# Cross attention on one Trainium2 core: seven block products in float32 replaced by three float32r products

## The chip, the core and the metric

The kernel runs on one core of a Trainium2 chip. The core has a matrix engine (TensorE, PE in the profile, with its weight loads listed apart as PEld), three engines for elementwise work (VectorE or DVE, ScalarE or ACT, GpSimd or POOL), a queue engine that issues DMA (SyncE or SP), an on-chip memory (SBUF) and eight accumulation banks (PSUM) of 512 float32 per partition. Each engine works through its own list of instructions in order and waits on semaphores for the others. The metric is the device time in microseconds of one execution; lower is better.

## The reference

For each of 32 batches, x and y are 256 channels by 1024 positions:

```python
x_q = jnp.einsum('oc,bcn->bno', w_qk, y)
x_k = jnp.einsum('oc,bcn->bon', w_qk, x)
x_v = jnp.einsum('oc,bcn->bon', w_v, x) + b_v[None, :, None]
energy = jnp.einsum('bnc,bcm->bnm', x_q, x_k)
attention = jax.nn.softmax(energy, axis=-1)
attention = attention / (1e-07 + attention.sum(axis=1, keepdims=True))
x_r = jnp.einsum('bcn,bnm->bcm', x_v, attention)
x_r = jax.nn.relu(jnp.einsum('oc,bcn->bon', w_t, x - x_r) + b_t[None, :, None])
return x + x_r
```

The energies are a 1024 by 1024 table per batch. Each row gets a softmax, then each column is divided by its sum S over the rows (plus 1e-7).

## The kernel before

Weights are folded once: G = w_qk^T w_qk is applied to x alone ("keys", tile `gf`), so that energy = y^T (G x); w_v and w_t are folded into one matrix, so that u = (w_t w_v x)^T ("values", tile `ut`). The output is then relu(w_t x - u attention + b_t) + x.

TensorE works in two ways. The energies use *float32r* operands, which the array multiplies in one pass at reduced precision; each operand is split into a high part, a low part and a mixed part (class `Split`, lines 243 to 282: `yf` and `gf`, three forms each), and three products are summed in PSUM. A row tile of 128 rows by 1024 columns takes 12 matmuls of 512 columns. All other products are full float32, which the profile shows as two matmul records each. To save some of them, keys, values and attention are computed by a scheme of seven block products instead of eight (class `Seven`, lines 293 to 350, with `Keys`, `Values` and `Attention`): the 2 by 2 blocks of each operand are added into sums (`summed`, `factors`, `mix`, `lefts`), and the seven products are combined afterwards (`combine`).

The order on PE, DVE, ACT and POOL is the order of the program text: class `InOrder` (line 62) chains each instruction behind the last one of its engine. DMA issues of SP are placed by the scheduler. One batch goes so:

- Energy, 8 row tiles n (lines 712 to 740): `first` and `second` on PE, `scaled` on ACT between them (it multiplies the sum of the first two forms in place by a constant), the row minimum `nm` on DVE, the exponential on ACT into the SBUF tile `e`, which holds all 8 rows, and `share` on DVE, which adds e times 1/rowsum into the column sums `acc`.
- Keys and values of the next batch (lines 742 to 767), then `columns` and `inverse` (lines 631 to 658), which turn `acc` into 1/S along the columns (tile `rc`).
- Attention (`Attention.run`, lines 557 to 595): `normal` multiplies all of `e` by 1/rowsum and by 1/S on DVE, `mix` forms the block sums `et` on DVE, PE multiplies them by `ur` (from `ut`, with sums `us` made on POOL), together with w_t times x (`xpart`), and DVE combines, adds x and stores.

Forms of the next batch's y and keys are made by ACT and by accumulating DMAs issued from POOL (`lower`, `mixed`), block sums of x by accumulating DMAs too (`summed`).

Of the kernel before, what the change touches and what calls it, by code (L numbers as in the profile page):

```python
# [17 lines left out]
def kernel(  # L18
# [11 lines left out]

# [12 lines left out]
    BIG = 3.0e38  # L53
    UP = 4096.0
    UNDER = 1.0 - 2.0**-13
    OVER = 1.0 + 2.0**-12

    const = ctx.enter_context(tc.tile_pool(name="const", bufs=1))
    xp = ctx.enter_context(tc.tile_pool(name="xp", bufs=2))
    ps_m = ctx.enter_context(tc.tile_pool(name="ps_m", bufs=1, space=bass.MemoryType.PSUM))  # L60

# [16 lines left out]
    pe, dve, act, pool = (InOrder(g) for g in (nc.tensor, nc.vector, nc.scalar, nc.gpsimd))  # L78

    banks = ps_m.tile([P, 8, MB], F32, name="banks")  # L80

    def bank(j):
        return banks[:, j]

    loaded = {}

    def load(b, pieces=1):
        to = xp.tile([P, KC, N], F32, tag="x", name=f"x_{b}")
        from_ = x[b].rearrange("(k p) n -> p k n", p=P)
        W = KC // pieces  # L90
        for j in range(pieces):
            nc.sync.dma_start(to[:, ts(j, W)], from_[:, ts(j, W)])
        loaded[b] = to

    def quarters(from_):

        return from_.rearrange("(k p) (h n) -> p k h n", p=P, h=MH)

    def corners(from_):

        q = quarters(from_)[:, 0, 0, :]
        return bass.AP(
            tensor=q.tensor, offset=q.offset, ap=[q.ap[0], [P * N + MB, 2], q.ap[-1]]
        )

    def accumulate(into, from_):
# [4 lines left out]
    ep = ctx.enter_context(tc.tile_pool(name="ep", bufs=1))  # L111
    scratch = ep.tile([P, 2, HT, MB], F32, tag="et", name="scratch").rearrange(
        "p j t m -> p (j t) m"
    )

    def room(j):
        return scratch[:, j, : KC * C].rearrange("p (k c) -> p k c", k=KC)

    wqk, wv, wt = room(0), room(1), room(2)
    ident = scratch[:, 3, :P]  # L120
    bv = scratch[:, 4, :KC].rearrange("p (k o) -> p k o", o=1)
    bvs = scratch[:, 5, : KC * P].rearrange("p (k n) -> p k n", k=KC)
    bt = const.tile([P, KC, 1], F32, name="bt")
    nbt = const.tile([P, KC, 1], F32, name="nbt")
    bu = const.tile([P, KC, P], F32, name="bu")
    for k, start in enumerate((nc.sync.dma_start, act.dma_start)):
        start(wqk[:, k], w_qk[ts(k, P)])
    load(0, KC)
    nc.sync.dma_start(wt, w_t.rearrange("(k p) c -> p k c", p=P))
    nc.sync.dma_start(bv, b_v.rearrange("(k p o) -> p k o", p=P, o=1))  # L130
    nc.sync.dma_start(wv, w_v.rearrange("(k p) c -> p k c", p=P))
    nc.sync.dma_start(bt, b_t.rearrange("(k p o) -> p k o", p=P, o=1))


    few = const.tile([P, P], F32, name="few")
    dve.memset(few, 0.0)
    behind = const.tile([P, 1], F32, name="behind")
    parts = const.tile([P, NB, NG + 1], F32, name="parts")
    dve.memset(parts[:, :, NG], EPS)
    idle = bank(7)  # L140
    for _ in range(5):
        pe.matmul(idle[:, :P], few, few, start=True, stop=True)
    make_identity(nc, ident)

    def lefts(name, ps, sign=1.0):


        w = const.tile([P, KC, C], F32, name=name)
        for k in range(KC):
            act.mul(w[:, k, :], ps[k][:, :C], sign)  # L150
        sums = const.tile([P, 4, P], F32, name=f"{name}s")
        s1, s2, s3, s4 = (sums[:, j] for j in range(4))

        def stt(out_, block, factor, other, op):
            dve.scalar_tensor_tensor(out_, block, factor * sign, other, ALU.mult, op)

        p11, p12, p21 = ps[0][:, :P], ps[1][:, :P], ps[0][:, P:C]
        a11, a12, a21, a22 = w[:, 0, :P], w[:, 1, :P], w[:, 0, P:], w[:, 1, P:]
        stt(s1, p21, 1.0, a22, ALU.subtract)
        stt(s3, p11, 1.0, a21, ALU.subtract)  # L160
        stt(s2, p11, -1.0, s1, ALU.add)
        stt(s4, p12, 1.0, s2, ALU.add)
        return w, (a11, a12, s4, a22, s1, s2, s3)


    pg = [bank(3 + i) for i in range(KC)]
# [5 lines left out]
    _, g_left = lefts("g", pg, UP)  # L172

    for k in range(KC):
        dve.tensor_scalar(bvs[:, k], few, bv[:, k], None, ALU.add)

    def turned_weights():

        pt = [bank(6 + i) for i in range(KC)]
        for i in range(KC):  # L180
            for k in range(KC):
                pe.transpose(pt[i][:, ts(k, P)], wt[:, k, ts(i, P)], ident)
        return lefts("wtT", pt)

    def value_weights(wtT):

        pw = [bank(4 + i) for i in range(KC)]
        for i in range(KC):
            for k in range(KC):
                pe.matmul(  # L190
                    pw[i][:, :C], wv[:, k, ts(i, P)], wtT[:, k, :], start=(k == 0), stop=(k == KC - 1)
                )
        return lefts("wvtT", pw, -1.0)[1]

    def value_bias(wtT):

        pb = bank(6)
        for k in range(KC):
            pe.matmul(pb[:, :C], bvs[:, k], wtT[:, k, :], start=(k == 0), stop=(k == KC - 1))
        act.mul(bu.rearrange("p k c -> p (k c)"), pb[:, :C], -1.0)  # L200
        act.mul(nbt[:, :, 0], bt[:, :, 0], -1.0)

    up = ctx.enter_context(tc.tile_pool(name="up", bufs=2))
    one = ctx.enter_context(tc.tile_pool(name="one", bufs=1))
    cp = ctx.enter_context(tc.tile_pool(name="cp", bufs=2))
    rowp = ctx.enter_context(tc.tile_pool(name="rowp", bufs=4))
    sp = ctx.enter_context(tc.tile_pool(name="sp", bufs=4))

    def temp(tag, name):
        return cp.tile([P, MB], F32, tag=tag, name=name)  # L210

    def matmul(into, lhs, rhs, onto=False):
        pe.matmul(into, lhs, rhs, start=not onto, stop=True, skip_group_check=onto)

    def value(v):

        return v.bitcast(F32)

    def summed(b):

        s = up.tile([P, 4, MB], F32, tag="xs", name=f"xs_{b}")
        t1, t3, t4, t2 = (s[:, j] for j in range(4))
        to = loaded[b]
        b11, b12 = to[:, 0, ts(0, MB)], to[:, 0, ts(1, MB)]
        b21, b22 = to[:, 1, ts(0, MB)], to[:, 1, ts(1, MB)]
        if b == 0:
            pool.tensor_tensor(t1, b11, b12, ALU.add)
            pool.tensor_tensor(t2, b22, t1, ALU.add)
            pool.tensor_tensor(t3, b12, b22, ALU.add)
            pool.tensor_tensor(t4, b21, t2, ALU.add)  # L230
            steps = []
        else:
            q = quarters(x[b])
            nc.sync.dma_start(s[:, :2], q[:, 0, 1:2, :].to_broadcast([P, 2, MB]))
            nc.sync.dma_start(s[:, 2:], q[:, 1])
            steps = [
                lambda: accumulate(s[:, :2], corners(x[b])),
                lambda: accumulate(s[:, 2:], s[:, 0:1].to_broadcast([P, 2, MB])),
                lambda: accumulate(t4, q[:, 1, 1]),
            ]  # L240
        return (b11, b21, b22, t4, t1, t2, t3), steps

    class Split:


        def __init__(self, name, b, by):
            self.name, self.b, self.by = name, b, by
            self.to = one.tile([P, 3, KC, N], F32R, tag=name, name=f"{name}_{b}")
            self.rows = {}

        def row(self, i):
            if i not in self.rows:
                self.rows[i] = rowp.tile([P, N], F32, tag="row", name=f"{self.name}r_{self.b}_{i}")
            return self.rows[i]

        def parts(self, i):

            high, low, both = (self.to[:, j, i] for j in range(3))
            act.mul(high, self.rows[i], UNDER * self.by)
            act.mul(low, value(high), -1.0 / self.by)  # L260
            act.mul(both, value(high), -1.0 / (UP * self.by))

        def high(self, i):
            act.mul(self.to[:, 0, i], self.rows[i], UNDER * self.by)

        def low(self, i):
            high, low = (self.to[:, j, i] for j in range(2))
            dve.scalar_tensor_tensor(
                low, value(high), -1.0 / self.by, self.rows[i], ALU.mult, ALU.add
            )  # L270

        def both(self, i):
            high, low, both = (self.to[:, j, i] for j in range(3))
            dve.scalar_tensor_tensor(
                both, value(high), -1.0 / (UP * self.by), value(low), ALU.mult, ALU.add
            )

        def lower(self, i):
            accumulate(value(self.to[:, 1, i]), self.rows[i])

        def mixed(self, i):
            accumulate(value(self.to[:, 2, i]), value(self.to[:, 1, i]))

# [196 lines left out]
    class Attention(Seven):  # L480
# [76 lines left out]
        def run(self, u, before=None, between=None):  # L557
# [7 lines left out]
            if u:  # L565
                u.c22()
# [288 lines left out]
```

## Time and profile before

| | |
|---|---|
| device time, median of 3 runs | 2095.8 us (2094.79 to 2096.62) |
| span of the profiled execution | 2094.2 us; no separate device time of that execution is given |
| TensorE clock granted | 0.999 of full |
| PE busy / PEld busy | 2080.7 / 1289.2 us |
| DVE / ACT / POOL busy | 1774.5 / 1145.9 / 674.7 us |
| DMA traffic | 306.04 MB, 170.68 MB of it in the queue that POOL feeds |

The span is the time from the first to the last instruction of one execution; a median a microsecond or two above it is the same time measured from outside. Busy time is the time in which an engine had a record open. In the profile `banks<-gf,yf` is an energy matmul, `banks<-e,ut`, `banks<-et,us`, `banks<-e,us` and `banks<-et,ut` are attention, `xs`, `x` with `g`, `gs` keys, with `wvtT`, `wvtTs` values, with `wtT`, `wtTs` the product w_t x. Nearly all lines read L73, because one helper issues every instruction; groups are told apart by their tiles.

### The profile page before, as it was taken

The page shows a single profiled execution, that of the slowest core. Times are in us where ns is not written, and L with a number is a line of the kernel's source. Part 1 is how long each engine was busy: PE and PEld are TensorE (multiplying, and loading weights), DVE is VectorE, ACT ScalarE, POOL GpSimd, SP SyncE. Part 2 cuts the span into 40 slices and gives each one's busy share as a digit, 9 for nine tenths or more (in the row PEclk, how much of TensorE's full clock was granted, in tenths as well). Part 3 has the DMA queues.
Part 4 walks back from the last instruction along what each step waited for, and adds up shares of the span by engine and source line. Part 5 has one row for each costly group of instructions (what it writes and reads, how often), then busy time and mean ns, then how long its engine had stood idle before and what let it go on. Part 6 is the DMA issues. An engine that isn't in the chain of part 4 may idle for free.

```text
span 2094.2 us, 21719 instructions
## 1 busy us (share of the span) xinstructions
PE 2080.7 (99%) x7586; PEld 1289.2 (62%) x7586; DVE 1774.5 (85%) x2264; ACT 1145.9 (55%) x1570; POOL 674.7 (32%) x574
## 2 busy tenths in 40 slices
PE   9999999999999999999999999999999999999998
PEld 6556666566665666556666556665566665666564
DVE  6898888998888988889888898888988888988898
ACT  5556554566455664546655556554566455664562
POOL 3322333323333133432333322333323333133321
PEclk9999999999999999999999999999999999999999
DMA  4766577665676656766558756577665776656740
GB/s 141 169 123 146 132 175 171 128 150 129 166 175 151 135 132 151 181 155 135 139 135 186 169 123 146 131 176 171 132 145 130 167 178 145 138 132 151 181 95 31
DMA packets 107789, 306.04 MB, mean 146 GB/s; under 512 B 10656, under 2 KB 11424, under 8 KB 107680
## 3 DMA queue, kind: packets, MB, share of 16 engines
q0 software_dynamic: 57040, 170.68, 44.5%
q1 hardware_dynamic: 50496, 133.85, 18.7%
q8 instruction: 60, 0.98, 0.2%
q14 instruction: 49, 0.40, 0.1%
q10 hardware_dynamic: 144, 0.13, 0.0%
HBM read 124.78 MB, written 33.55 MB: 76 GB/s over the span
## 4 chain that ended last, share of the span: by engine, by line
PE 72%; DVE 24%; issue 1%; DMA 0%; DVEq 0%; ACT 0%
PE banks L73 72%; DVE e L73 12%; DVE et L73 4%; DVE gfr L73 3%; DVE rc L73 2%; DVE sc L73 2%; DVE parts L73 1%; DVE acc L73 1%; DVE nm L73 0%; DMA gf<-gf 0%; DVEq L73 0%; DVE ri L73 0%; DVE z L73 0%; ACT ow L73 0%
## 5 line engine op out<-in xcount | busy, mean ns | idle before, releaser
L73 PE MATMUL banks<-gf,yf 128*128 128x512 f32 x3072 | 716.3, 394 | 0.3 <-DMA gf<-gf 0.3
L73 PEld LDWEIGHTS banks<-gf,yf 128*128 128x128 f32 x3072 | 576.2, 188 | 134.7 <-issue 15.5
L73 DVE TENSOR_REDUCE nm<-banks 128x1 f32<-128x1024 f32 x256 | 310.6, 1223 | 148.6 <-PE banks L73 136.1
L73 ACT ACTIVATE e<-banks,nm 128x1024 f32<-128x1024 f32 x256 | 287.0, 1121 | 134.5 <-DVE nm L73 134.5
L73 PE MATMUL banks<-et,us 128*128 128x512 f32 x768 | 353.9, 597 | 3.1 <-DVE et L73 1.4
L73 DVE SCALAR_TENSOR_TENSOR e<-e,ri,rc 128x512 f32<-128x512 f32 x512 | 347.4, 746 | 1.1
L73 ACT ACTIVATE banks<-banks 128x1024 f32<-128x1024 f32 (+1 forms) x288 | 264.1, 917 | 66.7 <-PE banks L73 66.6
L73 DVE SCALAR_TENSOR_TENSOR acc<-e,ri,acc 128x1024 f32<-128x1024 f32 x224 | 289.2, 1291 | 8.0
L73 PEld LDWEIGHTS banks<-et,us 128*128 128x128 f32 x768 | 143.2, 190 | 198.3 <-issue 161.7
L73 PE MATMUL banks<-e,ut 128*128 128x512 f32 x512 | 225.0, 592 | 0.9 <-DVE e L73 0.9
L73 POOL DMA_DIRECT2D yf<-yfr x62 | 53.1, 857 | 520.5 <-ACT yf L73 520.5
L73 ACT ACTIVATE z<-banks,bt 128x512 f32<-128x512 f32 x31 | 21.4, 689 | 338.5 <-DMA out_dram<-z 338.5
L73 PEld LDWEIGHTS banks<-e,ut 128*128 128x128 f32 x512 | 97.2, 190 | 123.7 <-issue 106.7
L73 DVE TENSOR_TENSOR et<-e 128x1024 f32<-128x1024 f32 x128 | 153.7, 1221 | 4.4
L73 POOL TENSOR_TENSOR ut<-ut,bu 128x1024 f32<-128x1024 f32 x64 | 154.6, 2501 | 0.3 <-ACT ut L73 0.3
L73 POOL DMA_DIRECT2D gf<-gf x62 | 53.1, 857 | 302.4 <-DMA gf<-gfr 257.7
L73 DVE SCALAR_TENSOR_TENSOR z<-z,x 128x512 f32<-128x512 f32 x96 | 134.6, 1403 | 3.3
L73 PE MATMUL banks<-e,us 128*128 128x512 f32 x256 | 125.3, 592 | 0.0
L73 ACT ACTIVATE gf<-gf 128x1024 fp32r<-128x1024 f32 x124 | 124.2, 1049 | 2.0
L73 ACT ACTIVATE yf<-yf 128x1024 fp32r<-128x1024 f32 x124 | 124.2, 1049 | 2.0
L73 POOL DMA_DIRECT2D xs<-xs x31 | 37.2, 1201 | 246.9 <-DMA xs<-in_x_dram 237.9
L73 PEld LDWEIGHTS banks<-wvtTs,xs 128*128 128x128 f32 x768 | 98.2, 192 | 29.6 <-issue 29.6
(104 smaller groups left out, 2617.0 us busy)
## 6 DMA issues: line engine op xcount, KB each, us to landing
yfr<-in_ctx_dram SPq DMA_DIRECT2D x64, 512.0 KB, 5.7
out_dram<-z SPq DMA_DIRECT2D x128, 256.0 KB, 3.5
x<-in_x_dram SPq DMA_DIRECT2D x31, 1024.0 KB, 7.5
xs<-in_x_dram SPq DMA_DIRECT2D x62, 512.0 KB, 5.0
yf<-yfr POOLq DMA_DIRECT2D x62, 512.0 KB, 5.2
yf<-yf POOLq DMA_DIRECT2D x62, 512.0 KB, 7.7
gf<-gfr POOLq DMA_DIRECT2D x62, 512.0 KB, 10.7
gf<-gf POOLq DMA_DIRECT2D x62, 512.0 KB, 5.2
```

The costliest lines, as they stand in the source:

```text
L73: self.last = getattr(self.engine, name)(*args, **kwargs)
```

## The change

The new kernel writes every product as three float32r products and drops the block scheme. Both operands of keys, values, w_t x, energy and attention now have three forms (HIGH, LOW, REST), and each product is HIGH x HIGH + REST x REST + LOW x LOW of suitably scaled forms, accumulated in one PSUM bank. Constants on either side carry the scales.

The division by S moves: attention multiplies u by the exponentials over the row sum alone, and 1/S is applied to the finished output columns (`divided`), together with a bias.

Exponentials stay in PSUM: `exp` writes in place over the energies, and the three forms of a row (`ef`, three buffers) and the column sum (`share`) are read from PSUM. Eight banks are four pairs: pairs 0 and 1 hold energy rows in turn (and keys and the first half of the values at the change of batch), pairs 2 and 3 the attention accumulators of the two output channel tiles (and the second half of the values, and w_t x). As attention no longer needs S, it follows the rows: after energy tile n, PE does attention of tile n - 2 (`attention`).

The forms of y are made per half of 512 positions (`Queries`), with two accumulating DMAs; those of x by ACT, POOL and one accumulating DMA per channel tile; those of keys and values out of PSUM by ACT and two DVE operations (`Right`); those of a row by ACT, DVE and one POOL addition (`low`). x is loaded a second time for the output.

The core of the diff, new code:

```python
class Right:                      # forms of keys and of values
    def high(self):
        act.mul(self.forms[0], self.p, 1.0 / UP)
    def low(self):
        dve.scalar_tensor_tensor(
            self.forms[1], value(self.forms[0]), -UP, self.p, ALU.mult, ALU.add)
    def rest(self):
        dve.scalar_tensor_tensor(
            self.forms[2], self.p, 1.0 / UP, value(self.forms[1]), ALU.mult, ALU.subtract)

# class Batch
def channels(self, p, w, i):      # keys(i) with gw, straight(c) with tw
    for h in range(MH):
        for j in ORDER:           # HIGH, REST, LOW
            for k in range(KC):
                matmul(p[:, h], w[:, j, k, ts(i, P)], self.xf[:, j, k, ts(h, MB)], ...)

def values(self, q):
    p = pair(2 if q else 3 if self.b == 0 else self.at)
    for t in range(HT):
        for j in ORDER:
            for k in range(KC):
                matmul(p[:, t // 2, ts(t % 2, C)], self.xf[:, j, k, ts(q * HT + t, P)], vw[:, j, k], ...)
...
def place(self, n):
    return pair((self.at + 1 + n) % 2)
def lowest(self, n):
    dve.tensor_reduce(low, flat(self.place(n)), AX.X, ALU.min)
def exp(self, n):
    p = flat(self.place(n))
    act.activation(p, p, AF.Exp, bias=self.row[n], scale=-1.0, accum_out=rs)
def high(self, n, h):
    act.mul(self.ef[n][:, HIGH, ts(h, MB)], self.place(n)[:, h], self.row[n])
def rest(self, n, h):
    dve.scalar_tensor_tensor(
        f[:, REST], self.place(n)[:, h], self.row[n], value(f[:, HIGH]), ALU.mult, ALU.subtract)
def scaled(self, n):
    act.mul(self.ef[n][:, LOW], value(self.ef[n][:, HIGH]), 1.0 / UP)
def low(self, n):
    pool.tensor_tensor(f[:, LOW], value(f[:, LOW]), value(f[:, REST]), ALU.add)
def share(self, n):
    for h in range(MH):
        dve.scalar_tensor_tensor(a, p[:, h], ri, a, ALU.mult, ALU.add)
def forms(self, n):
    for h in range(MH):
        self.high(n, h)
        self.rest(n, h)
    self.scaled(n)
    self.low(n)
def attention(self, n):           # 12 matmuls of 512 columns
    for c in range(KC):
        for h in range(MH):
            for j in ORDER:
                matmul(pair(2 + c)[:, h], u[:, j, ts(c, P)], self.ef[n][:, j, ts(h, MB)], ...)
def divided(self, c):
    dve.scalar_tensor_tensor(
        self.z[:, c], flat(pair(2 + c)), ubias[:, c], self.rc, ALU.add, ALU.mult)
...
# the row loop; what the turn of the batch does stands around it
for n in range(2, NT):
    if n > 2:
        cur.energy(n)
    cur.lowest(n)
    if n > 2:
        cur.share(n - 1)
    cur.exp(n)
    cur.recip(n)
    cur.forms(n)
    cur.attention(n - 2)
    if more and n == 2:
        nxt.x_high(0)
        nxt.x_rest(0)
    elif more and n == 3:
        nxt.x_high(1)
        nxt.x_rest(1)
        nxt.x_scaled(0)
    elif more and n == 4:
        nxt.x_scaled(1)
        nxt.x_low(0)
        nxt.x_low(1)
    if last and n == 5:
        last.relu(1)
        last.put(1)
```

In the turn, the order on PE is: attention 5, keys 0, attention 6, keys 1, attention 7, first half of the values, energy 0, second half of the values, w_t x for channel tile 0, energy 1, w_t x for tile 1, energy 2, attention 0, energy 3, and so on. On DVE it is: forms and share of row 7, `low` and `rest` of keys 0, `columns`, `inverse`, `low` and `rest` of keys 1, `divided` twice, then row 0 of the next batch with the forms of the values between its steps.

More of the change, by code (lines that the diff above doesn't have):

```diff
@@ L167 @@
+    ys = {}
+    cur = Batch(0)
+    for q in range(3):
+        ys[q] = Queries(q) if q < 2 else None
+    pg = [banks[:, i] for i in range(KC)]
     for i in range(KC):
@@ L207 @@
[L207 to L241, printed above, removed]
@@ L785 @@
[L785 to L824 removed]
+        nxt = Batch(b + 1)
@@ new lines @@
+        first = b == 0
+        v0 = cur.values(0)
+        v0.high()
+        if first or not more:
+            v0.low()
+        if first:
+            v1 = cur.values(1)
+        cur.energy(0)
+        cur.lowest(0)
+        if first:
+            v0.rest()
+        else:
+            if more:
+                v0.low()
+            v1 = cur.values(1)
+        cur.exp(0)
+        cur.recip(0)
+        v1.high()
+        if first:
+            cur.energy(1)
+            for q in (1, 2):
+                ys[q].low()
+        else:
+            v0.rest()
@@ new lines @@
+        cur.forms(0)
+        if first:
+            v1.low()
+            v1.rest()
+        if more:
+            cur.straight(0)
+            cur.straight_out(0)
+        if not first:
+            last.relu(0)
+            last.load_out()
+            last.put(0)
+        cur.share(0)
+        if not first:
+            v1.low()
+            cur.energy(1)
+        cur.lowest(1)
+        if not first:
+            v1.rest()
+        cur.exp(1)
+        cur.recip(1)
+        if more:
+            cur.straight(1)
+            cur.straight_out(1, ts(0, 1))
@@ new lines @@
+        for h in range(MH):
+            cur.high(1, h)
+            cur.rest(1, h)
+        if more:
+            cur.straight_out(1, ts(1, 1))
+        cur.scaled(1)
+        cur.low(1)
+        if more:
+            nxt.load_x()
+        cur.energy(2)
+        cur.share(1)
+        for n in range(2, NT):
[22 more added lines that the diff above has]
+                last.put(1)
@@ new lines @@
+        if more:
+            k0 = nxt.keys(0)
+        else:
+            cur.load_out()
+            cur.straight(0, nxt.at)
+            cur.straight_out(0)
+        cur.share(NT - 1)
+        if more:
+            k0.high()
+            k0.low()
+            k0.rest()
+        cur.columns()
+        cur.inverse()
+        cur.attention(NT - 2)
+        later = [q for q in (2 * b + 3, 2 * b + 4) if q < B * MH]
+        if more:
+            k1 = nxt.keys(1)
+        else:
+            cur.straight(1, 1 - nxt.at)
+            cur.straight_out(1)
@@ new lines @@
+        for q in later:
+            ys[q] = Queries(q)
+            ys[q].high()
+            ys[q].minus()
+            if more and q == later[0]:
+                k1.high()
+            ys[q].rest()
+            ys[q].scaled()
+        if more:
+            k1.low()
+            k1.rest()
+        cur.attention(NT - 1)
+        if more:
+            for c in range(KC):
+                cur.divided(c)
+                cur.joined(c)
+        else:
+            cur.finish()
+        for q in later:
+            ys[q].low()
```

842 lines of the change are left out of this document (284 added, 558 removed).

## The prediction

> **What bounds the kernel now.** I read the page's busy line first, then its slices of the span, then the chain:
>
> ```profile
> span 2094.2 us, 21719 instructions
> PE 2080.7 (99%) x7586; PEld 1289.2 (62%) x7586; DVE 1774.5 (85%) x2264; ACT 1145.9 (55%) x1570; POOL 674.7 (32%) x574
> ...
> PE   9999999999999999999999999999999999999998
> ...
> DVE  6898888998888988889888898888988888988898
> ...
> PEclk9999999999999999999999999999999999999999
> ...
> PE 72%; DVE 24%; issue 1%; DMA 0%; DVEq 0%; ACT 0%
> PE banks L73 72%; DVE e L73 12%; DVE et L73 4%; DVE gfr L73 3%; DVE rc L73 2%; DVE sc L73 2%; DVE parts L73 1%; DVE acc L73 1%; DVE nm L73 0%; DMA gf<-gf 0%; DVEq L73 0%; DVE ri L73 0%; DVE z L73 0%; ACT ow L73 0%
> ```
>
> PE is full in all 40 slices at full granted clock. DVE is second, and the 24% of the chain that runs over it (`e`, `et`, `gfr`, `rc`) is work that PE's own list happens to cover, since PE has no gap there. A batch costs 2080.7/32 = 65.0 us of PE. So the question is how long PE's new list is, and then whether the other engines, rearranged, still keep PE fed.
>
> **The price of a matmul.**
>
> ```profile
> L73 PE MATMUL banks<-gf,yf 128*128 128x512 f32 x3072 | 716.3, 394 | 0.3 <-DMA gf<-gf 0.3
> L73 PE MATMUL banks<-e,ut 128*128 128x512 f32 x512 | 225.0, 592 | 0.9 <-DVE e L73 0.9
> L73 PEld LDWEIGHTS banks<-wvtTs,xs 128*128 128x128 f32 x768 | 98.2, 192 | 29.6 <-issue 29.6
> ```
>
> The first row is the energies, float32r (the type printed is f32). One matmul lasts 394 ns from start to result, but they overlap: busy time over count is 233 ns. Of that, the drain of the last one in each of 32 stretches, (394 - 233) x 32 = 5 us, overlaps what follows: 711/3072 = 0.2315 us each, with the small hand-over waits of the energy stage in it. The second row is full float32: two records per product, 225.0/512 = 0.44 us each, 0.88 per product. Three float32r products cost 0.69 against 0.88; the block scheme had made eight float32 products into seven, 0.77 each. So the new form is about 10% cheaper on all but the energies, which stay 96 matmuls per batch.
>
> New per batch: energy 96, attention 8 x 12 = 96, keys 24, w_t x 24, all of 512 columns: 240 x 0.2315 = 55.6 us. Values are 48 matmuls of 256 columns, a shape that the trace lacks. Half of 0.2315, 0.116, is its lower end. Its upper end is 0.192, the length of one weight load (third row), if loads of that length were not hidden. But in that row, whose matmuls have only 128 columns, 768 loads are busy for 98.2 us, 0.128 each: loads overlap each other and length is not pace. I take the middle of 0.116 and 0.128, 0.122: 5.9 us. PE's list is 61.4 us per batch, and over 32 batches 7680 x 0.2315 + 1536 x 0.122 = 1965 us.
>
> The Trainium skill, TensorE: Matmul & The Clock Gate, section Back-to-back issue gap, gives N/2.4 + 2.5 ns, 216 ns for 512 columns and 109 for 256. The trace has 231 for exactly this operand type, so the measurement decides. By the page's figure the list would be 7680 x 0.2157 + 1536 x 0.109 = 1824 us.
>
> **Load of the other engines.** Rows for the new steps:
>
> ```profile
> L73 DVE TENSOR_REDUCE nm<-banks 128x1 f32<-128x1024 f32 x256 | 310.6, 1223 | 148.6 <-PE banks L73 136.1
> L73 DVE SCALAR_TENSOR_TENSOR e<-e,ri,rc 128x512 f32<-128x512 f32 x512 | 347.4, 746 | 1.1
> L73 DVE SCALAR_TENSOR_TENSOR acc<-e,ri,acc 128x1024 f32<-128x1024 f32 x224 | 289.2, 1291 | 8.0
> L73 DVE SCALAR_TENSOR_TENSOR z<-z,x 128x512 f32<-128x512 f32 x96 | 134.6, 1403 | 3.3
> L73 ACT ACTIVATE e<-banks,nm 128x1024 f32<-128x1024 f32 x256 | 287.0, 1121 | 134.5 <-DVE nm L73 134.5
> L73 ACT ACTIVATE z<-banks,bt 128x512 f32<-128x512 f32 x31 | 21.4, 689 | 338.5 <-DMA out_dram<-z 338.5
> L73 ACT ACTIVATE yf<-yf 128x1024 fp32r<-128x1024 f32 x124 | 124.2, 1049 | 2.0
> L73 POOL TENSOR_TENSOR ut<-ut,bu 128x1024 f32<-128x1024 f32 x64 | 154.6, 2501 | 0.3 <-ACT ut L73 0.3
> L73 POOL DMA_DIRECT2D yf<-yfr x62 | 53.1, 857 | 520.5 <-ACT yf L73 520.5
> ```
>
> DVE per row: minimum 1.22; `rest` and `share`, four operations of 512 out of PSUM, between 0.61 (half of the minimum, which reads 1024 out of PSUM) and 0.75 (the same operation out of SBUF): I take 0.75, as it is the same operation; a reciprocal, some 0.15. That is 4.4 us, x 8 = 35. Per batch besides: eight operations of 1024 for keys and values at 1.29, `divided` 2.6, `columns` 1.2, `inverse` 3.3 (`rc`, `sc` and `parts` have 5% of the chain, 105 us, over 32): 17. Sum 52 of 61.4 us. ACT: per row 1.2 + 2 x 0.69 + 1.05 = 3.6, x 8 = 29; forms of y 6.3, of x 4.2, of keys and values 4.4, `straight_out` 2.4, relu 2.1: 48. POOL: 8 `low`, 2 `x_rest`, 2 `joined`, 2 `put` of 2.5 us = 35, and six DMA issues of 0.86 = 5: 40. None is the bound by load. What goes (block sums, `normal`, the constant `scaled` in PSUM) lay under PE's cover and gains nothing itself; it only makes room.
>
> **Hand-overs.** What PE can wait for is PSUM: row n + 2 overwrites row n's pair, so its first matmul waits for the first half of `share(n)`, which on DVE stands behind the minimum of row n + 1. How late DVE starts after PE: at least the drain, 0.16 us; at most that and all of the idle time before a minimum, 148.6/256 = 0.58, so 0.74. I take 0.65, near the top, as the minima had little else ahead of them. From the end of energy tile n + 1: 0.65 + 1.22 + 0.75 = 2.62 us, plus an estimated 0.05 for the hand-over back; attention on PE covers 12 x 0.2315 = 2.78. It fits with 0.1 to spare, so I add nothing at these five places per batch; with 0.74 it still just fits.
>
> Row n's own chain, from the end of its tile: minimum to 1.9, exponential to 3.1, reciprocal (behind `share(n - 1)`) to 3.55, `high` to 4.25, `rest` twice to 5.8; DVE's next minimum is due at 5.56 + 0.65 = 6.2. It fits. `scaled` ends near 6, POOL's `low` at 8.5, and attention n starts at 11.1.
>
> The turn of the batch, from the end of energy tile 7. PE unhindered: attention 5, keys 0, attention 6, keys 1, attention 7, 2.78 each, half of the values 2.9: energy 0 could start at 16.8. It needs keys 1 out of PSUM. DVE: `rest` of row 7 to 5.8, `share` 7.3, keys 0 `low` and `rest` 9.9, `columns` 11.1, `inverse` 14.4, keys 1 `low` and `rest` 17.0: 0.2 late, I take 0.3. `divided` ends at 19.6; w_t x, which reuses that pair, starts at 22.8. Next tight place: beside rows 0 and 1, DVE makes the values' forms, and runs late into row 2. Followed the same way, `share(1)` ends at 35.8, minimum 2 at 37.0, `rest(2)` at 40.6, minimum 3 at 41.8, half of `share(2)` at 42.6, against 42.3 at which PE wants energy 4: 0.3 us, and 0.9 if a half-row of `high` or `share` slips by one operation. I take 0.6. Waits per batch 0.9, x 31 = 28 us; ends 0 and 3.
>
> The x forms end in an accumulating DMA (`x_low`) issued by POOL behind `low(4)`, near 56 on this clock; keys of the next batch read it at 66. Landing, by its like:
>
> ```profile
> yf<-yf POOLq DMA_DIRECT2D x62, 512.0 KB, 7.7
> gf<-gfr POOLq DMA_DIRECT2D x62, 512.0 KB, 10.7
> gf<-gf POOLq DMA_DIRECT2D x62, 512.0 KB, 5.2
> ```
>
> Hidden at 5.2 or 7.7 (out of SBUF, like this one), 0.7 us late at 10.7. On SP's queue the loads of y and x wait for buffers that `put` and the copies free, long before use; nothing PE needs soon hangs on them.
>
> **The sum.** Head: to the first energy tile DVE does ten operations of 1.29 and 18 on 256 columns at some 0.47 (746 less half of the step to 1291), 21 us, from about 8.5 (x landing, 7.5 in its row, and a copy):
>
> ```profile
> x<-in_x_dram SPq DMA_DIRECT2D x31, 1024.0 KB, 7.5
> out_dram<-z SPq DMA_DIRECT2D x128, 256.0 KB, 3.5
> ```
>
> 30 us, in which PE does keys and values (11.5): 18 of idle. Tail: the last store, 3.5, and two operations: 5. First and last batch, whose order lacks some cover: 4. Total 1965 + 18 + 28 + 5 + 4 = 2020 us of span; the median stands 1.6 above the profiled span now, so **2022**.
>
> **Rivals.**
> 1. DVE is late throughout turn and rows, 3 us per batch instead of 0.9: 2022 + 31 x 2.1 = 2087. For it: margins of 0.1. Against: a row asks 4.4 us of DVE in 5.6, so lateness is made up.
> 2. Slower: POOL's additions are held up by DVE. At 3.5 us instead of 2.5, the five of rows 2 to 4, from 40 on, put `low(4)` at 57.7 and `x_low` at 59.5; landing in 10.7, keys 0 gets it at 70.2 instead of 66.3, 3.9 us per batch: 2022 + 31 x 3.9 = 2143. From 2.4 us per batch, additions of about 3.2, it is slower than now. For it: DVE's `z<-z,x` took 1403 ns where the like-sized `e` took 746, so something holds such operations up. Against: the new row operations of DVE have only one operand in SBUF. The Trainium skill, SBUF — State Buffer, section Who interferes with whom, has GpSimd locked out only against DVE operations with two SBUF inputs or in a two-port mode; by that rule the additions stay at 2.5. The 1403 agrees, as `z<-z,x` has two.
> 3. Values at the length of a weight load: + 1536 x 0.07 = 108: 2130. Against: 0.128 above.
> 4. Matmuls of 512 columns at 0.216: 2022 - 141 = 1881. Against: 0.2315 for the same type now.
>
> **Chances.** Main case 0.61 (own range 1965 to 2055: from no waits, - 28, values at 0.116, - 9, and no idle in the head, - 18, up to 2 us of waits per batch, + 34), rival 1 0.21, rival 2 0.10, rival 3 0.05, rival 4 0.03. The range 1965 to 2090 leaves out rivals 2, 3 and 4. Within 0.2% is about what a measurement of this kernel can tell; faster 0.84, same 0.02, slower 0.14 (rivals 2, 3).
>
> **What would show it.** Right: 61 to 64 us per batch; `ef` and `gf` matmuls at 0.23, `vw` at 0.12; PE's idle put down to DVE (`acc`, `gf`), about 1 us per batch. Wrong: idle before `ef` matmuls released by POOL or before `xf` ones by DMA (rival 2), `vw` at 0.18 or more (rival 3), a wait of PE for `acc` in every row (rival 1).

## The result, and the profile after

The changed kernel takes 2000.29 us (median, 1999.9 to 2001.84) against 2095.62 us for the kernel before, measured beside it: a ratio of 0.9547, 95% interval 0.9533 to 0.956, so 4.5% faster. The prediction was 2022.

The page of the changed kernel (all instructions now read L66, the line of the helper that issues them): busy times, PE's slices, the granted clock, the chain.

```profile
span 2000.1 us, 25163 instructions
...
PE 1978.3 (99%) x9254; PEld 1634.8 (82%) x9254; DVE 1564.5 (78%) x2180; ACT 1462.3 (73%) x1894; POOL 1245.5 (62%) x638
...
PE   8999999999999999999999999999999999999997
...
PEclk9999999999999999999999999999999999999999
...
PE 96%; DVE 2%; ACT 1%; DMA 0%; issue 0%; SPq 0%; DVEq 0%
```

PE is as full as before, so the gain came from where the prediction looked for it: PE's own list. What changed beside it is the chain. Before, 24% of it ran over DVE; now 96% is PE alone and DVE has 2%, although DVE has 78% of the span in work. From 54 to 1937 us, in all batches but the first and the last, the profile shows no wait of PE.

The groups that carry the sum, same page (busy us, mean ns of one, then idle time ahead of them and its releaser):

```profile
L66 POOL TENSOR_TENSOR ef<-ef 128x1024 fp32r<-128x1024 f32 x256 | 617.0, 2410 | 487.9 <-ACT ef L66 386.3
L66 PE MATMUL banks<-gf,yf 128*128 128x512 f32 x3072 | 756.5, 395 | 3.8 <-DVE acc L66 2.8
L66 PE MATMUL banks<-ef,uf 128*128 128x512 f32 x3072 | 756.4, 394 | 1.0 <-ACT banks L66 1.0
...
L66 DVE SCALAR_TENSOR_TENSOR ef<-banks,ri,ef 128x512 fp32r<-128x512 f32 x512 | 360.9, 746 | 215.5 <-ACT ef L66 215.5
...
L66 DVE SCALAR_TENSOR_TENSOR acc<-banks,ri,acc 128x512 f32<-128x512 f32 x448 | 313.7, 742 | 0.0
...
L66 PE MATMUL banks<-vw,xf 128*128 128x256 f32 x1536 | 193.7, 282 | 0.0
L66 PE MATMUL banks<-xf,tw 128*128 128x512 f32 x768 | 187.0, 392 | 1.2 <-ACT xe L66 1.2
L66 PE MATMUL banks<-xf,gw 128*128 128x512 f32 x768 | 186.8, 393 | 0.0
...
xf<-xf POOLq DMA_DIRECT2D x62, 512.0 KB, 5.9
```

The energies alternate with other work now, so each tile is a stretch of its own with its own drain at the end: 756.5/3072 = 0.246 us contains an overlap of some 0.16 us per 12 matmuls and is not the pace. The pace is read from the starts of the tiles in the timeline of the trace, here over one batch, in my table:

| PE's tile | starts, us | to the start of the next |
|---|---|---|
| first half of the values, 24 x 256 columns | 1007.72 | 2.86 |
| energy 0 | 1010.58 | 2.77 |
| ... | | |
| attention 3 | 1044.08 | 2.80 |
| energy 6 | 1046.88 | 2.80 |
| ... | | |
| keys 0 | 1058.07 | 2.73 |
| attention 6 | 1060.80 | 2.79 |
| ... | | |
| first half of the values, next batch | 1069.12 | 2.86 |

From values to values: 1069.12 - 1007.72 = 61.40 us. The kernel before takes 64.67 from the first energy tile of a batch to that of the next (the 65.0 of the prediction, busy time over 32, holds its ends too). A tile of energy or attention takes 2.80 us (0.233 each), one of keys 2.73 (0.228), 24 matmuls of the values 2.86 (0.119). Attention stands at the same price per matmul as the energies and the keys at nearly the same: the price that float32r had in the old energy stage now holds for everything. That is the gain: 3.27 us a batch are 105 us over 32, of which head, tail and the first and last batch take 9 back.

### The profile page after: what moved, and what is told of

It reads as the page before. It is cut to its first block, busy times and chain, and to the rows that moved or that the text cites. A ratio compares the mean times of both kernels' runs of the same rounds, so it can differ in the third digit from the quotient of the medians.

```text
span 2000.1 us, 25163 instructions
## 1 busy us (share of the span) xinstructions
PE 1978.3 (99%) x9254; PEld 1634.8 (82%) x9254; DVE 1564.5 (78%) x2180; ACT 1462.3 (73%) x1894; POOL 1245.5 (62%) x638
## 4 chain that ended last, share of the span: by engine, by line
PE 96%; DVE 2%; ACT 1%; DMA 0%; issue 0%; SPq 0%; DVEq 0%
PE banks L66 96%; DVE nm L66 0%; DVE z L66 0%; DVE ef L66 0%; ACT banks L66 0%; DMA stage<-in_L_xattn_w_t_dram 0%; DVE acc L66 0%; DVE uf L66 0%; ACT yf L66 0%; ACT ef L66 0%; ACT uf L66 0%; ACT gf L66 0%; SPq L113 0%; DVE ri L66 0%; ACT wtT L66 0%
## 5 line engine op out<-in xcount | busy, mean ns | idle before, releaser
L66 POOL TENSOR_TENSOR ef<-ef 128x1024 fp32r<-128x1024 f32 x256 | 617.0, 2410 | 487.9 <-ACT ef L66 386.3
L66 PE MATMUL banks<-gf,yf 128*128 128x512 f32 x3072 | 756.5, 395 | 3.8 <-DVE acc L66 2.8
L66 PE MATMUL banks<-ef,uf 128*128 128x512 f32 x3072 | 756.4, 394 | 1.0 <-ACT banks L66 1.0
L66 PEld LDWEIGHTS banks<-ef,uf 128*128 128x128 f32 x3072 | 576.6, 188 | 139.0 <-ACT banks L66 1.4
L66 PEld LDWEIGHTS banks<-gf,yf 128*128 128x128 f32 x3072 | 574.7, 188 | 139.6 <-issue 2.3
L66 DVE SCALAR_TENSOR_TENSOR ef<-banks,ri,ef 128x512 fp32r<-128x512 f32 x512 | 360.9, 746 | 215.5 <-ACT ef L66 215.5
L66 ACT ACTIVATE banks<-banks,nm 128x1024 f32<-128x1024 f32 x256 | 277.9, 1085 | 318.3 <-DVE nm L66 316.3
L66 DVE TENSOR_REDUCE nm<-banks 128x1 f32<-128x1024 f32 x256 | 312.8, 1222 | 127.0 <-PE banks L66 125.1
L66 ACT ACTIVATE ef<-banks,ri 128x512 fp32r<-128x512 f32 x512 | 324.4, 686 | 54.2 <-DVE ri L66 53.6
L66 DVE SCALAR_TENSOR_TENSOR acc<-banks,ri,acc 128x512 f32<-128x512 f32 x448 | 313.7, 742 | 0.0
L66 ACT ACTIVATE ef<-ef 128x1024 fp32r<-128x1024 f32 x256 | 272.6, 1065 | 7.1
L66 POOL DMA_DIRECT2D yf<-in_ctx_dram x63 | 76.8, 1218 | 221.2 <-ACT yf L66 219.0
L66 PEld LDWEIGHTS banks<-vw,xf 128*128 128x128 f32 x1536 | 192.2, 191 | 5.5
L66 PE MATMUL banks<-vw,xf 128*128 128x256 f32 x1536 | 193.7, 282 | 0.0
L66 PE MATMUL banks<-xf,tw 128*128 128x512 f32 x768 | 187.0, 392 | 1.2 <-ACT xe L66 1.2
L66 PE MATMUL banks<-xf,gw 128*128 128x512 f32 x768 | 186.8, 393 | 0.0
L66 PEld LDWEIGHTS banks<-xf,gw 128*128 128x128 f32 x768 | 145.2, 189 | 32.0
L66 PEld LDWEIGHTS banks<-xf,tw 128*128 128x128 f32 x768 | 142.1, 188 | 31.6 <-ACT xe L66 1.7
L66 POOL TENSOR_TENSOR z<-z,xe 128x1024 f32<-128x1024 f32 x62 | 147.6, 2396 | 19.3 <-DVE z L66 19.3
L66 POOL TENSOR_TENSOR z<-z,xo 128x1024 f32<-128x1024 f32 (+1 forms) x64 | 152.6, 2385 | 9.2 <-ACT z L66 9.2
L66 POOL TENSOR_TENSOR xf<-x,xf 128x1024 fp32r<-128x1024 f32 x62 | 149.7, 2415 | 0.0
L66 ACT ACTIVATE gf<-banks 128x1024 fp32r<-128x1024 f32 x64 | 65.8, 1028 | 91.5 <-PE banks L66 91.5
```

Source lines behind the costliest of these rows:

```text
L66: self.last = getattr(self.engine, name)(*args, **kwargs)
```

## The experiments

All are edits of the changed kernel. Each was run beside the kernel before (2093.85 for the first four, 2094.84 for the next two, 2094.58 for the last three); the changed kernel's 2000.3 is from its own comparison. The first six kernels were run once each, the last three four or five times. Times of one kernel differ by up to 2.8 us (the kernel before, 2093.84 to 2096.62), so smaller differences tell nothing.

### How much room DVE has in a row

The forecast rested on cover of 2.78 us against a need of 2.67. To measure the room, DVE was given one more operation in rows 3 to 7, ahead of `share`: a minimum over half a row, or over a whole one, which nobody reads.

```diff
             cur.lowest(n)
             if n > 2:
+                spare = sp.tile([P, 1], F32, tag="nx", ...)
+                dve.tensor_reduce(spare, cur.place(n - 1)[:, 1], AX.X, ALU.min)   # e1
+                dve.tensor_reduce(spare, flat(cur.place(n - 1)), AX.X, ALU.min)   # e2
                 cur.share(n - 1)
```

> One more minimum over half a row (512 columns of PSUM, about 0.66 us of DVE's pace, its result unused) stands ahead of share in rows 3 to 7. Theory A (PE's list is the time; DVE starts 0.2 us after PE's last slot, so the first half of share ends about 2.05 us after it and 2.8 us of attention leave 0.7 us to spare): the time stays, 1998 to 2006. Theory B (the prediction's hand-over of 0.65 us, 0.1 to spare, with the waits merely not shown): 0.55 us at five places in 31 batches, +85, 2085.

> As the run with half a row, with a minimum over the whole row: 1.2 us more of DVE ahead of share in rows 3 to 7. Theory A: 0.45 us too much at each of five places, 72 us in all, and DVE's own load of a row goes to 5.5 of 5.6 us, so lateness is no longer made up: 2060 to 2110. Theory B: 1.05 us at each, +165, 2165. If neither margin matters, 2000.

Measured: 2018.99 and 2096.59. The busy times and the energies' row of the half-row kernel, then the energies' row and the other rows that changed of the full-row kernel:

```profile
PE 1995.2 (99%) x9254; PEld 1623.1 (80%) x9254; DVE 1649.1 (82%) x2340; ACT 1460.5 (72%) x1894; POOL 1244.1 (62%) x638
...
L66 PE MATMUL banks<-gf,yf 128*128 128x512 f32 x3072 | 764.8, 398 | 6.0 <-DVE acc L66 4.2
```

```profile
L66 PE MATMUL banks<-gf,yf 128*128 128x512 f32 x3072 | 771.5, 400 | 47.8 <-DVE acc L66 45.7
...
L66 PE MATMUL banks<-xf,gw 128*128 128x512 f32 x768 | 188.9, 395 | 9.9 <-DVE acc L66 9.9
...
L66 DVE TENSOR_REDUCE nx<-banks 128x1 f32<-128x1024 f32 x160 | 194.2, 1214 | 0.0
```

The half row took DVE's busy time from 1564.5 to 1649.1, 85 us, and cost 19: it uses up the room and a little more. The full row added 1.21 us in 160 places and cost 96, half of its own length each time: 55.6 us (45.7 + 9.9) as waits, 53 of them new, 160 x 0.16 = 26 as the time that the last matmul ahead of each wait needs to finish, which a wait exposes, and 15 (771.5 against 756.5) as energy tiles that start and are then held up once more. So the room is about 0.6 us a row, neither the 0.1 of the prediction nor plenty, and an overrun of 0.6 more in five rows is worth the whole gain. My expectation for the half row (up to 2006) missed by 13 us; the full row fell into its range.

Both sides of the same place in the changed kernel's timeline (start, length, engine, operation; in brackets the idle time ahead), first PE's attention 3 and energy 6, then DVE's minimum of row 5 and the two operations of `share(4)`:

```profile
1044.08 2.96 PE L66 MATMUL banks<-ef,uf 128*128 128x512 f32 x12
1046.88 2.96 PE L66 MATMUL banks<-gf,yf 128*128 128x512 f32 x12
...
1044.28 1.22 DVE L66 TENSOR_REDUCE nm<-banks 128x1 f32<-128x1024 f32 x1 [0.59 <-PE banks L66]
1045.42 1.40 DVE L66 SCALAR_TENSOR_TENSOR acc<-banks,ri,acc 128x512 f32<-128x512 f32 x2
```

The attention tile starts when the energy tile has been issued, 1044.08; the minimum starts 0.20 us later. That is the hand-over which I had put at 0.65; it is 0.20 at all 159 minima that DVE had to wait for. The first half of `share` is done near 1046.16, and PE wants the pair at 1046.88: 0.7. Where PE does wait, it starts 0.05 us (full row) to 0.15 us (two products, below) after that half is done, which leaves the 0.6.

### What PE's list is worth

Two edits of w_t x, a stage in which PE waits for nothing: as 8 plain float32 matmuls instead of 24 float32r ones, and with LOW x LOW left out.

```diff
 def straight(self, c, to=3):
-    self.channels(pair(to), tw, c)          # HIGH, REST, LOW
+    # e3: value(tw[:, HIGH, ...]) x value(xf[:, HIGH, ...]), float32
+    # e4: j in (HIGH, REST)
```

> w_t x alone goes back to plain float32 matmuls, eight of 512 columns per batch on the HIGH forms, in place of 24 float32r ones (the LOW and REST products are left out, so the output is not the reference's in the last digits). Theory A (PE's list is the time): 8 x 0.86 = 6.88 us against 24 x 0.228 = 5.47 us, +1.41 us in 31 to 32 batches, +44: 2044, 2038 to 2050. Rival (the turn of the batch is set by DVE and ACT, PE only waits unseen): 2000.

> w_t x with two products in place of three (LOW x LOW is left out, so the output is not the reference's). Theory A: 8 matmuls of 0.228 us fewer per batch, -58: 1942, or up to 1970 if the shorter cover in the turn opens waits of up to 1 us per batch. Rival (turn set by DVE and ACT): 1990 to 2000.

Measured: 2038.53 (38.2 more) and 1980.99 (19.3 less). Of the kernel with float32 products and of the one with two products:

```profile
PE 2015.1 (99%) x8998; PEld 1586.6 (78%) x8998; DVE 1566.7 (77%) x2180; ACT 1464.0 (72%) x1894; POOL 1241.9 (61%) x638
...
L66 PE MATMUL banks<-xf,tw 128*128 128x512 f32 x512 | 230.2, 592 | 1.2 <-ACT xe L66 1.2
```

```profile
L66 PE MATMUL banks<-gf,yf 128*128 128x512 f32 x3072 | 758.8, 395 | 34.3 <-DVE acc L66 32.1
...
L66 PE MATMUL banks<-xf,tw 128*128 128x512 f32 x512 | 129.7, 396 | 2.1 <-ACT xe L66 2.1
```

One direction is the list and nothing else: the row of w_t x grew by 230.2 - 187.0 = 43 us, all of busy PE by 36.8 (2015.1 against 1978.3; records of neighbouring groups overlap), and the time by 38. It also prices the gain of the change: per product of 512 columns, 38 us over 32 x 8 is 0.15, which three float32r matmuls beat one float32 product by, in the same place and kernel; the prediction's rows had given 0.88 - 0.69 = 0.19. The other direction isn't: 187.0 - 129.7 = 57 us of PE were saved and 19 came out. 32.1 us stand as a wait for `acc`, 33 times, some 0.98 us each: energy 4 waiting for `share(2)`. 29 of them are new; with 32 exposed ends of 0.16 (5 us) and 2 us in which energy tiles are held up once more (758.8 against 756.5) they make 36 of the missing 38. This is the place that the prediction named as the second tight one of the turn. The two tiles of w_t x lie ahead of it, so shortening them takes away DVE's cover. In the changed kernel the first half of `share(2)` is done at 1035.04 and energy 4 starts at 1035.69: that is 0.65 us of the 8 x 0.228 = 1.82 cut, and the wait of 0.98 with its exposed end of 0.16 is the rest. 1981 lies between my two ranges. The waits of up to 1 us per batch that I allowed for (1970) did open, with the exposed ends on top; the rival is wrong for the changed kernel, where PE has that 0.65 us to spare, but beyond the 0.65 DVE does set the turn.

### Whether the loads of weights count

PE loads weights for every matmul (PEld 1634.8 us busy beside it). With the loop over column halves innermost, two matmuls in a row have the same weights.

```diff
-for h in range(MH):
-    for j in ORDER:
-        for k in range(KC):
+for j in ORDER:
+    for k in range(KC):
+        for h in range(MH):
             matmul(p[:, h], w[:, j, k, ts(i, P)], self.xf[:, j, k, ts(h, MB)], ...)
```

> Keys, w_t x and attention issue their two column halves one after the other for the same stationary operand (the loop over halves innermost); the number of matmuls and the products are the same, energies keep their order. If the 0.228 to 0.233 us of a float32r matmul, against 0.213 for 512 columns at the streaming rate, hold a cost of changing the weights that is saved when they stay, up to 144 matmuls x 0.5 x 0.03 us per batch, -70: 1930 to 1990. If every matmul loads its weights again whatever came before: 1998 to 2004.

Measured: 2002.05. Its busy times:

```profile
PE 1978.3 (99%) x9254; PEld 1634.0 (82%) x9254; DVE 1563.6 (78%) x2180; ACT 1464.1 (73%) x1894; POOL 1246.0 (62%) x638
```

PE is busy for 1978.3 us as before, and there are as many loads as before, x9254: one for each matmul, also where two in a row have the same weights. Nothing is gained or lost that this run can tell.

### Why the exponentials stay in PSUM

Rival 2 of the prediction was a clash of DVE and POOL. The nearest version of the kernel in which it should occur writes the exponentials to SBUF (into the REST slot of `ef`), so that `share` reads two operands from SBUF. To keep the slot free for `rest`, `share(n)` then has to come ahead of `forms(n)`; a second kernel makes that change of order alone.

```diff
 # e6 only
-act.activation(p, p, AF.Exp, ...)
+act.activation(self.ef[n][:, REST], p, AF.Exp, ...)   # and high, rest, share read it there
 # e6 and e7
 def forms(self, n):
+    self.share(n)
     for h in range(MH):
         self.high(n, h)
         self.rest(n, h)
 ...
-    cur.share(n - 1)        # behind the next row's minimum
```

> The part 'exponentials stay in PSUM' undone alone: the exponential writes into SBUF (into the REST form of the row, rounded to float32r, so the output differs in its last digits), its forms and the column sum read it there, and the column sum is taken before the forms of the same row. DVE's rest and share then have two operands in SBUF. Theory (Trainium skill, SBUF — State Buffer, Who interferes with whom: such operations and GpSimd exclude each other): POOL's additions go from 2.41 to 3 us or more and DVE's operations of 512 from 0.74 to 1 us or more, so DVE's row goes from 4.4 to over 5.6 us: slower, 2050 to 2200. Rival (PSUM or SBUF is the same to DVE; only the early release of PSUM counts, which nothing waits for): 1998 to 2006.

> The order of e6_exp_sbuf alone: each row's share comes ahead of its own rest on VectorE instead of behind the next row's minimum, and the exponentials stay in PSUM as in the changed kernel. Theory A (what cost 127 us in e6_exp_sbuf was the place of the exponentials, which made share an operation with two operands in SBUF that POOL's additions hold up): acc operations back at some 742 ns mean, none above 0.8 us beside an addition, and the time near 2000; between 1998 and 2015, as share(n) then ends some 4.3 us after its energy tile (0.2 + 1.22 + 1.1 + 0.3 + 1.5) where TensorE needs the pair 8.4 us after it. Theory B (it was the order: rest, and with it scaled, low and attention, come 1.5 us later): a time of 2060 or more with acc at 742 ns.

Measured: 2127.52 for both edits (127 more), 2021.06 for the order alone (ratio to before 0.9647, 0.9634 to 0.966). Page of the first:

```profile
L66 POOL TENSOR_TENSOR ef<-ef 128x1024 fp32r<-128x1024 f32 x256 | 614.8, 2401 | 647.5 <-DVE ef L66 491.4
L66 PE MATMUL banks<-ef,uf 128*128 128x512 f32 x3072 | 772.4, 396 | 53.4 <-POOL ef L66 53.4
L66 PE MATMUL banks<-gf,yf 128*128 128x512 f32 x3072 | 758.7, 395 | 55.0 <-DVE gf L66 53.7
...
L66 DVE SCALAR_TENSOR_TENSOR acc<-ef,ri,acc 128x512 f32<-128x512 f32 x448 | 504.5, 1166 | 7.8
```

Page of the second:

```profile
L66 PE MATMUL banks<-gf,yf 128*128 128x512 f32 x3072 | 759.0, 395 | 18.0 <-DVE gf L66 16.8
...
L66 DVE SCALAR_TENSOR_TENSOR acc<-banks,ri,acc 128x512 f32<-128x512 f32 x448 | 315.7, 746 | 7.8
```

And one stretch of the first kernel's timeline: POOL starts an addition, `x_rest`, at 1040.28, which lasts 2.41 us; DVE starts the two operations of a `share` at 1040.42, and they last 3.49.

The same `share` takes 746 ns with one operand in SBUF and 1166 on average with two; beside the addition of POOL, which had started first, a pair of them takes 3.49 us instead of 1.40. The mean hides two cases. In the first kernel's trace, 127 of the 448 operations start while an addition of POOL is under way and take 2228 ns on average; the other 321 take 745. In the changed kernel 354 of the 448 start so and take 742. So it takes both, two operands in SBUF and a running addition. POOL's additions keep their 2.40 us. DVE is the one that waits, and PE waits for what comes after it: the keys' forms (53.7 us) and POOL's `low`, which stands behind DVE's `rest` (53.4).

So of the 127 us about 21 are order and 106 the place of the exponentials, if the order costs the same in both kernels. That isn't shown: with the order alone, ACT's `high` starts only when the first half of `share` is done, after 1.10 us of idle time in a row instead of 0.29, and in the first kernel it doesn't wait for it. So the part of the place may be larger. My expectation for the order alone ended at 2015, and 2021 lies above it. As `high` waits, `rest` comes later, the minimum of row 7 behind it (in the batch near 1000 us) starts 1.25 us after its tile instead of 0.20, DVE reaches the forms of keys 0 1.3 us later, and energy 0 waits 16.8/32 = 0.5 us in each batch for the forms of keys 1. That is the first tight place of the turn that the prediction had named.

### Whether the alternation is the cover

Two energy tiles, then two attention tiles. Every engine has the same instructions.

```diff
-            cur.attention(n - 2)
+            if n % 2:
+                cur.attention(n - 3)
+                cur.attention(n - 2)
```

> In the row loop attention no longer alternates with energy tiles: two energy tiles, then two attention tiles. The same instructions on every engine. Theory A (the attention tile between two energy tiles is what covers minimum and share, 0.20 + 1.22 + 0.75 us and a hand-over back of some 0.05): energies 5 and 7 now wait 2.2 us each for share, 2 x 2.2 x 32 = 141 us, and energy 3 up to 1.2 us: 2141 to 2178, and 2120 at the lowest. Rival (the balance over a pair of rows is enough, the order within it not): 2000 to 2015.

Measured: 2222.04 (ratio to before 1.0607, 1.0593 to 1.0622), slower than the kernel before, and 44 more than the upper end I gave. Page:

```profile
PE 2052.9 (92%) x9254; PEld 1668.1 (75%) x9254; DVE 1561.8 (70%) x2180; ACT 1463.6 (66%) x1894; POOL 1239.7 (56%) x638
...
L66 PE MATMUL banks<-gf,yf 128*128 128x512 f32 x3072 | 813.7, 417 | 153.1 <-DVE acc L66 152.1
```

The waits are those expected: 2.07 us twice a batch (energies 5 and 7) and 0.43 once (energy 3), 152 us against 3 in the changed kernel, about 149 of the 222. The timeline of the trace and the granted clock in windows of 1 us show where another part went:

| tile | starts, us | wait ahead of it | duration | granted clock |
|---|---|---|---|---|
| energy 4 | 1010.08 | none | 2.96 | 1.00 |
| energy 5 | 1015.11 | 2.07, for `acc` | 4.58 | 0.50 from 1016 to 1019, 1.00 from 1020 |
| attention 2 and 3 | 1019.53 | none | 5.74 | 1.00 |
| energy 6 | 1025.11 | none | 2.97 | 1.00 |
| energy 7 | 1030.15 | 2.07, for `acc` | 3.02 | 1.00 |

Behind the first wait of 2.07 us in the batch, the tile takes 4.58 us instead of 2.96, at a granted clock of 0.50; behind the second, equally long, it takes 3.02. Of 66 waits of 2 us or more in the execution, 33 are followed by a tile at half clock, 1.6 us longer: 53 us. Waits and half clock make 202 of 222; 93 waits x 0.16 = 15 are exposed ends of matmuls; 5 are left over. So the alternation is the cover, and its absence costs the waits and then half as much again.

### A shorter head

The forms of w_t, needed only for w_t x, were made after the forms of the first keys.

```diff
-    tw = weights("tw", pt, 1.0)              # ahead of cur.keys(0)
+    tw = weights("tw", [wtT[:, k] for k in range(KC)], 1.0)   # behind k1.rest()
```

> The forms of w_t are made after those of the first batch's keys instead of ahead of them, out of the SBUF copy of w_t. Theory A (in the head VectorE's six operations on 256 columns, some 0.47 us each, stand ahead of the keys' forms for which TensorE waits): the first energy tile some 2 to 2.8 us earlier than 27.84 us, and 1997.5 to 1999 where the changed kernel has 2000.3. Rival (the head hangs on loads of x and y, not on VectorE): first energy tile at 27.8 and 2000.3.

Measured: 1999.8 us (1999.45 to 2001.48), ratio to before 0.955 (0.9537 to 0.9563), against 0.9547 (0.9533 to 0.956): no difference that these runs can tell. In the profiled execution the first energy tile did start at 24.90 instead of 27.84, and the span was 2.4 us shorter. But 1.2 of that is w_t landing earlier, as the transposes that wait for it start at 7.80 instead of 8.96, and 0.6 came back as a wait of w_t x for its bank. The rest doesn't show theory A either. In both kernels DVE sits idle ahead of the first keys' forms (2.41 us in the changed kernel, 1.75 here), because it waits, through ACT, for PE's keys. And PE's granted clock was 0.50 from 11.2 to 18.0 us in the changed kernel and from 8.9 to 12.3 here, so the 24 matmuls of the keys took 7.05 us there and 5.55 here. Inconclusive: what the head could still give isn't shown.

## Why the prediction was right, and where it was off

- **What bounds.** Right. PE full before and after, and an edit that lengthens only PE's list (float32 w_t x) comes out in the time nearly whole.
- **PE's list.** 61.4 us per batch predicted, 61.40 measured. Three small errors cancel, so the agreement to the hundredth is luck: energies and attention take 0.233 instead of 0.2315 (192 x 0.0015 = + 0.3 us per batch), keys and w_t x 0.228 (48 x 0.0035 = - 0.2), values 0.119 instead of 0.122 (- 0.1). By the Trainium skill, TensorE: Matmul & The Clock Gate, section Back-to-back issue gap, the matmul of 512 columns would take 216 ns, by a formula that the section gives for an isolated matmul; this trace has 228 to 233 in long stretches at a granted clock of 1.00, so rival 4 fell with it. Why keys are 2% cheaper than energies wasn't tried.
- **Load of the others.** Right: `rest` 746 ns and `share` 742 out of PSUM, as the same operation out of SBUF; POOL's addition 2410; DVE 1564.5/32 = 49 us per batch against 52, ACT 46 against 48, POOL 39 against 40.
- **Hand-overs: the step that failed.** "I take 0.65, near the top" was the mis-sized term. The trace has 0.20, near the lower end of 0.16 to 0.74. The idle time before a minimum in the old kernel was not latency but real waiting, for PE to finish the tile: 134 of the 148.6 us stand ahead of the first three of a batch's eight minima, as in this batch of its timeline.

```profile
1004.43 1.22 DVE L73 TENSOR_REDUCE nm<-banks 128x1 f32<-128x1024 f32 x1 [1.70 <-PE banks L73]
1007.15 1.23 DVE L73 TENSOR_REDUCE nm<-banks 128x1 f32<-128x1024 f32 x1 [1.50 <-PE banks L73]
...
1009.87 1.23 DVE L73 TENSOR_REDUCE nm<-banks 128x1 f32<-128x1024 f32 x1 [0.64 <-PE banks L73]
...
1012.59 1.22 DVE L73 TENSOR_REDUCE nm<-banks 128x1 f32<-128x1024 f32 x1
```

The mis-sized hand-over accounts for less than half of the lateness that did not come. Counted from energy tile 7 as in the prediction, DVE is done with keys 1 at 15.9 us instead of 17.0, and with the first half of `share(2)` at 41.2 instead of 42.6. 0.45 us of each is the hand-over. The rest is in steps put 0.1 to 0.3 us too long each (the reciprocal, `rest`, the forms of keys, `inverse`), in part because whole records were added up: DVE's next operation starts before the record of the one ahead has ended (1.14 us after the start of a minimum of 1.22). So the turn's 0.3 and 0.6 us of lateness become 0.8 us to spare at energy 0 and 0.65 at energy 4, and the 28 us of waits don't occur. The places were right: the order-only and the two-product kernels put a wait at exactly these two.

- **x_low and the landings.** Right: 5.9 us, hidden; no `xf` matmul waits for DMA.
- **Ends.** Head: 27.84 - (5.5 + 5.7) = 16.6 us without keys and values on PE against 18. First and last batch: 1.2 (`xe`) + 2.8 (`acc`) + 1.0 + 1.0 (`banks`, `uf`) = 6 against 4. Tail: 10.6 us from the last matmul to the end of the span against 5; I had counted a store and two operations, but `finish` is a row of ten operations on DVE, five for each output tile, and those of the second tile come behind the first's. Sum of the measured terms: 1965 + 16.6 + 0 + 10.6 + 6 = 1998.2 of 2000.1.
- **The difference.** From the predicted span of 2020 to the profiled one of 2000.1 it is - 28 from waits, + 6.2 from the ends, and 1.9 that no term has. The profiled execution took 2001.84 us, 1.7 more than its span where 1.6 was assumed; the median happens to be 1.5 lower.
- **Rivals.** 1 (DVE late): didn't happen, but the full-row minimum shows it to be real and near, 1.2 us of DVE away in five rows. 2 (POOL held up): didn't happen; additions took 2.41 us. The rule of the Trainium skill, SBUF — State Buffer, section Who interferes with whom, held in both directions: no clash with `share` and `rest` reading PSUM, a clash as soon as `share` had two inputs in SBUF. Who is held up was DVE, not POOL as the rival had it, since POOL's addition was under way first. The section says that too: the order of issue decides who waits. The prediction's own case against the rival read half of this: `e<-e,ri,rc` at 746 ns has two operands in SBUF as well. In the old kernel none of its 512 operations runs beside an addition of POOL; of the 96 `z<-z,x`, the 61 that start during one take 1810 ns on average and the other 35 take 692. 3 (values at load length): 0.119, no.

## What to carry to other kernels

Price PE's list with the matmul of the same operand type in the kernel's own trace, from start to start of long stretches; that alone gave this result to 2%. Idle time in front of an instruction is an upper bound on a hand-over, and taking a value near it overstated the waits; look for the same hand-over at a place where the waiting engine had nothing else to do. Records of one engine overlap, so measure a chain of its operations from start to start. When the other engines are at 60 to 80% and PE has no gap, order is what is tight: before shortening PE's work somewhere, or moving a step on DVE, look which wait that work was covering.

## What the hardware showed that was not expected

- A wait of PE of 2.07 us was enough to halve the granted clock for 3.41 us, in 33 of 66 cases: in a steady batch at the first such wait and not at the one 15 us later. Waits of 0.98 us (two products, 33 times) and of up to 1.7 us (exponentials in SBUF, 32 times at energy 0, for the forms of keys 1) left the mean clock at 0.996 and 0.997; with the 2.07 us waits it was 0.971.
- What sets apart the waits of the same length stands in the traces. In all eleven the granted clock changes only at multiples of 3.413 us from its first change. From 30 us to the last matmul, half clock followed each 3.41 us stretch between these points that held 1.92 us or more of a wait of PE (33 with two energy tiles in a row, two with the full-row minimum, one with two products), and none that held 1.87 or less. The first wait of a batch falls whole into one stretch, 2.07 us; the second is cut by a boundary, mostly into some 0.87 and 1.20. A batch of that kernel lasts 68.2 us, close to 20 stretches (68.27), so the same wait is hit again and again. The Trainium skill, TensorE: Matmul & The Clock Gate, section The HAM clock gate, has half clock after an idle window of about 3.4 us; the length agrees, but here 1.92 us of waiting within such a window were enough.
- DVE's operation with two operands in SBUF waited for POOL's addition to end, 3.49 us for a pair instead of 1.40, while POOL lost nothing. With one operand in PSUM it wasn't touched (742 ns).
- An exponential written in place in PSUM took 1085 ns where the one from PSUM to SBUF took 1121 before and 1118 in the kernel with exponentials in SBUF: the place that avoids the clash is no dearer for ACT.
